# Two-layer graph network: another order of work between the layers, with the first block's layer-1 values in it

## The chip, the core and the metric

The kernel runs on one core of a Trainium2 chip. A core has a matrix engine (PE, with its weight loads listed as PEld), a vector engine (DVE), a scalar engine (ACT), a general engine (POOL) and a sync engine (SP) that only issues DMAs and waits. The metric is the time on the device in microseconds, the median of several runs.

## What is computed

Eight graphs ("batches") of 2048 nodes with 256 features share one 0/1 adjacency matrix. Cut to what matters, the reference is:

```python
# layer 0: attention in chunks of 256 keys, 4 heads of 64
h = relu(layernorm(x))
q, k, v = h @ Wq.T + bq, h @ Wk.T + bk, h @ Wv.T + bv
scores = clip(q @ k.T / 8, -10, 10); scores = where(adj == 0, -10, scores)
ctx = sum over chunks of softmax(scores within the chunk) @ v
o = ctx @ Wo.T + bo + h
x = x + layernorm(o) * gamma + beta
# layer 1: graph attention
h = relu(layernorm(x)); g = h @ W
e = leaky_relu(g @ a1 [:, None] + g @ a2 [None, :]); e = where(adj == 0, -1e9, e)
x = x + relu(softmax(e) @ g)
```

Everything is float32.

## The kernel before, in words

A batch is split into four blocks of 512 nodes, a block into four tiles of 128. Engines run their instructions in the order in which the program emits them (the schedule is written out by hand); waits between engines are put in where data, or a buffer's slot, is needed.

**Attention** of a batch is 32 steps, eight key chunks for each of the four query blocks. A step has two halves, `begin` and `end`, numbered 2f and 2f+1. Other work is hung on a half as a "piece" (`at(n, ...)`): pieces marked `first` run at its start, pieces marked `pe` at a set point among the matrix products, the others in between.

**A block between the layers** is the class `Between`: `output` and `take` (output projection, plus the residual), `stats`, `power`, `shift`, `scaled`, `gamma`, `add` (layer norm, then the sum into `x4`), then for layer 1 `stats1`, `power1`, `shift1`, `norm1` (layer norm and Relu), `turn1` and `keep1` (transposes on PE, copies by ACT into a tile `hT`), `values` and `keep` (the products with W and with a1 and a2; ACT copies them into `g`, DVE copies the two node values into `sd`). `ends(0)` is the two transposes with their copies, `ends(1)` the four value tiles with theirs. `beside` says at which half each of these runs for blocks 0 to 2; block 0 runs all of them within attention, block 1 (`low`) up to its transposes, block 2 (`mid`) up to `add`. The rest of `low` and `mid`, and all of block 3 (`last`), comes in the **layer change** after attention (lines 986 to 1066).

**The next batch's projections** (`ahead`, class `Projection`) share the layer change: for each of its blocks a load, `norm` (Relu on ACT), `turn` (transposes; the first copy by DVE, the second by ACT), `qk` (four groups of products, evicted by ACT) and `values` (two groups, evicted by DVE). The last batch has no next one. There the first products of layer 1 are taken early: `weights(i)` makes a group of four weight tiles on DVE (L758 and L764), `early(i)` multiplies them with `g` (L781).

**Layer 1** (`Layer1`) then runs 16 groups of weights and products: four target blocks times four groups of source tiles, with `finish` and `store` per block.

Buffers that matter here: in the layer change the small matrix results (`ps_m`) take four banks in turn, two called `n` and two called `t`; a bank is free once its result is evicted, by every reader. Tiles of normed rows (`hn`) have five slots, transposed ones (`hT`) two, per-block scales (`rn`) four.

The attention chain of the last block ends with a scaling on DVE (L470, `prod`) and a gather DMA from POOL (L475), behind which POOL still has the second `add` of block `mid` (L621) and a `beta` of `last` (L617).

Of the kernel before, what the change touches and what calls it, by code (L numbers as in the profile page):

```python
# [28 lines left out]
def gnn_two_layers(  # L29
# [18 lines left out]
    nc = tc.nc  # L48
# [7 lines left out]
    TB = NB // P  # L56
    NNB = N // NB
# [104 lines left out]
    def pe(piece):  # L162

        piece.kind = "pe"
        return piece
# [90 lines left out]
    def norm_stats(t4, mv, tiles):  # L256
        for t in tiles:
            stats = small.tile([P, 6], F32, tag="stats", name="stats")
            nc.vector.bn_stats(stats, t4[:, t, :])
            nc.vector.bn_aggr(mv[:, t, :], stats)  # L260
# [12 lines left out]
    def norm_tiles(tag, bufs):  # L273
        mv = small.tile([P, TB, 2], F32, tag="mv", name="mv")
        rn = small.tile([P, 2, TB], F32, tag=tag, name=tag, bufs=bufs)
        return mv, rn
# [19 lines left out]
    class Projection:  # L296
# [31 lines left out]
        def take(self, nb, c):  # L328
            if c == 0:
                nc.vector.tensor_copy(self.hT[nb][:, 0, :], self.pt.pop(c))  # L330
            else:
                nc.scalar.activation(self.hT[nb][:, 1, :], self.pt.pop(c), AF.Copy)
# [225 lines left out]
    class Between:  # L558
# [23 lines left out]
        def take(self, t2):  # L582
            if t2 == 0:
                self.o4 = work.tile([P, TB, F], F32, tag="o4", name="o4", bufs=1)
                self.mv, self.rn = norm_tiles("rn", 4)
            nc.vector.tensor_tensor(
                self.o4[:, 2 * t2:2 * t2 + 2, :], self.pp[t2].rearrange("p (i f) -> p i f", i=2),
                self.hn0[t2], op=ALU.add,
            )
# [32 lines left out]

        def stats1(self, tiles):
            if tiles[0] == 0:
                self.mv1, self.rn1 = norm_tiles("rn", 4)
            norm_stats(self.x4, self.mv1, tiles)

        def power1(self):
# [42 lines left out]
                    self.values(t)  # L671
                    self.keep(t)

        def beside(self):

            todo = {
                -3: [self.load],
                3: [lambda: self.residual(0)],
                4: [lambda: self.residual(1)],
                5: [lambda: self.bias(0)],  # L680
                6: [lambda: self.bias(1)],
                8: [pe(lambda: self.output(0)), pe(lambda: self.output(1)), lambda: self.beta(0)],
                9: [first(lambda: self.take(0)), first(lambda: self.take(1)), lambda: self.stats([0, 1])],
                10: [lambda: self.stats([2]), lambda: self.beta(1)],
                11: [lambda: self.stats([3])],
                12: [self.power],
                13: [self.shift],
                14: [lambda: self.scaled(range(TB))],
                15: [lambda: self.gamma(0)],
                16: [lambda: self.gamma(1)],  # L690
                18: [lambda: self.add(0)],
                20: [lambda: self.add(1)],
            }

            def at(n, *pieces):
                todo.setdefault(n, []).extend(pieces)

            if self.nb == NNB - 2:
                return todo
            for t in range(TB):  # L700
                at(21 + t, lambda t=t: self.stats1([t]))
            at(25, self.power1)
            at(26, self.shift1)
            at(27, lambda: self.norm1(0))
            at(28, lambda: self.norm1(1))
            if self.nb == 0:
                for c in range(FC):
                    at(32, pe(lambda c=c: self.turn1(c)))
                    at(33, first(lambda c=c: self.keep1(c)))
                for t in range(TB):  # L710
                    at(36 + t // 2 * 2, pe(lambda t=t: self.values(t)))
                    at(37 + t // 2 * 2, first(lambda t=t: self.keep(t)))
            return todo


    class Layer1:
# [37 lines left out]
        def weights(self, nb, j4):  # L754
            w = work.tile([P, 4, NB], F32, tag="e", name="w", bufs=5)
            for i in range(4):
                j = 4 * j4 + i
                nc.vector.tensor_scalar(  # L758
                    w[:, i, :], self.src[nb], self.cd[:, 0, j:j + 1], self.cd[:, 1, j:j + 1],
                    op0=ALU.mult, op1=ALU.max,  # L760
                )
                if i % 2:
                    two = w[:, i - 1:i + 1, :]
                    nc.vector.scalar_tensor_tensor(  # L764
                        two, bounds1[nb][:, j - 1:j + 1, :], 0.0, two, op0=ALU.is_gt, op1=ALU.mult
                    )
            return w
# [44 lines left out]
    STEPS2 = 2 * STEPS  # L812
# [91 lines left out]
    for b in range(B):  # L904
        sd = small.tile([P, 2, NT], F32, tag="sd", name="sd", bufs=2)
        sums = small.tile([P, NNB, FC], F32, tag="sums", name="sums", bufs=2)
        blocks = [Between(nb, projs[b], att, sd, sums) for nb in range(NNB)]
        low, mid, last = blocks[NNB - 3:]
        ahead = projs.get(b + 1)
        one = Layer1(b, blocks, sd, sums)  # L910
        pieces1 = [(nb, j4) for nb in range(NNB) for j4 in range(NT // 4)]
        ws, accs = {}, {}
        todo = {}

        def at(n, *pieces):
            todo.setdefault(n, []).extend(pieces)
# [4 lines left out]
        def early(i):  # L921
            one.products(accs[0], ws.pop(i), i)
# [2 lines left out]
            of[nb] = fetch_bounds(nb)  # L925

        for nb in range(NNB - 1):
            for n, pieces in blocks[nb].beside().items():
                at((nb + 1) * PER + n, *pieces)
        if b == 0:  # L930
            for n, pieces in once.items():
# [2 lines left out]
            for nb in range(NNB):  # L934
                n = 12 * nb + 5
# [20 lines left out]
        if ahead:  # L956
            at(STEPS2 - 14, lambda: ahead.load(0))
            at(STEPS2 - 13, lambda: ahead.load(1))
            at(STEPS2 - 11, lambda: ahead.norm(0, 0))
            at(STEPS2 - 10, lambda: ahead.norm(0, 1))  # L960
            for c in range(FC):
                at(STEPS2 - 2, pe(lambda c=c: ahead.put(0, c)))
                at(STEPS2 - 1, first(lambda c=c: ahead.take(0, c)))
            at(STEPS2 + 2, pe(lambda: ahead.tiles()), pe(lambda: ahead.qk(0, 0, ps_h)), lambda: ahead.norm(1, 0))
            at(STEPS2 + 3, pe(lambda: ahead.qk(0, 1, ps_h)), lambda: ahead.norm(1, 1))
        else:
            at(STEPS2 - 1, lambda: one.targets(0, TB))
            at(STEPS2, pe(lambda: one.sources(0)))
            at(STEPS2 + 3, lambda: weights(0))
        turn_about[0] = False  # L970
        for n in sorted(todo):
            if n < 4:
# [10 lines left out]
        assert not todo  # L983


        low.ends(1)
        if ahead:
            ahead.load(2)
            ahead.turn(1, 0)
            ahead.turn(1, 1)  # L990
        mid.stats1(range(TB))
        mid.power1()
        mid.shift1()
        if ahead:
            ahead.values(0)
        else:
            accs[0] = one.accumulators(0)
            early(0)
        mid.norm1(0)
        mid.norm1(1)  # L1000
        last.output(0)
        last.output(1)
        last.take(0)
        last.take(1)
        if ahead:
            ahead.norm(2, 0)
            ahead.norm(2, 1)
        else:
            one.targets(TB, 2 * TB)
            weights(1)  # L1010
        mid.ends(0)
        if ahead:
            ahead.qk(1)
        else:
            early(1)
        last.stats(range(TB))
        last.power()
        last.shift()
        last.scaled(range(TB))
        mid.ends(1)  # L1020
        if ahead:
            ahead.load(3)
            ahead.turn(2, 0)
            ahead.turn(2, 1)
            ahead.values(1)
        else:
            one.targets(2 * TB, 3 * TB)
            weights(2)
            early(2)
        last.adder = nc.vector  # L1030
        for t2 in range(2):
            last.gamma(t2)
            last.add(t2)
        last.stats1(range(TB))
        last.power1()
        last.shift1()
        if ahead:
            ahead.norm(3, 0)
            ahead.norm(3, 1)
            ahead.qk(2)  # L1040
        last.norm1(0)
        last.norm1(1)
        if ahead:
            ahead.values(2)
        last.ends(0)
        if ahead:
            ahead.turn(3, 0)
            ahead.turn(3, 1)
        last.ends(1)
        one.total()  # L1050
        if ahead:
            ahead.qk(3, 0)
            one.targets()
            one.sources(0)
            one.sources(1)
            ahead.qk(3, 1)
            weights(0)
            one.mean()
            weights(1)
            ahead.values(3)  # L1060
        else:
            one.targets(3 * TB, NT)
            one.sources(1)
            weights(3)
            one.mean()
            weights(4)

        far = projs[b + 2] = Projection(b + 2) if b + 2 < B else None
        for i, (nb, j4) in enumerate(pieces1):
# [19 lines left out]
            if far and i in (1, 3, 6, 9):  # L1089
                n = (1, 3, 6, 9).index(i)  # L1090
# [45 lines left out]
```

## Time and profile before

| what | value |
|---|---|
| median of three runs | 3699.47 us (3697.77 to 3701.71) |
| the profiled run | 3696.62 us, span of the core 3694.8 us |
| mean granted clock of PE | 0.995 |
| instructions | 99356 |
| attention of batch 1, from its first product after the layer-1 products (L416) to its last | 556.87 to 830.81 us |
| layer change, from the last attention product (L416) to the first layer-1 product (L781), batch 0 | 377.75 to 436.84 us |
| layer 1 of batch 0, first to last product | 436.84 to 555.20 us |

A line of the page's first part gives an engine's busy time, its share of the span and its instructions. A line of waits reads: the instruction that waited, by engine, output and line; whom it waited for; the total in us, how many times, and the longest. A line of the timeline reads: start, duration, engine, line, operation, output and inputs, shapes, how many merged, and in brackets the engine's idle time before it and who ended it. PE's ends are modelled, so two products that follow each other overlap in these lines; their starts are what counts.

### The profile page before, as it was taken

Reading aid. Unit: us, or ns where it says so; the run is one execution under the profiler, and the core shown is the slowest. Engines: PE = TensorE matmul, PEld = TensorE weight load, DVE = VectorE, ACT = ScalarE, POOL = GpSimd, SP = SyncE. Lnnn points to the kernel's source line nnn. Section 1 sums busy time; section 2 is a strip of 40 time slices with the busy share of each in tenths; the row PEclk is TensorE's granted clock in tenths of the full one; section 3 lists DMA queues with packets and bytes.
Section 4 is the critical chain, followed back from the end, with each engine's and each line's share of the span. In section 5 each row is a group of like instructions: output and inputs, shape, how many; then the busy total and the mean of one; then the engine's idle time right before and its main releaser. Section 6 shows DMA issues by size and latency. Waiting matters only on the chain.

```text
span 3694.8 us, 99356 instructions
## 1 busy us (share of the span) xinstructions
PE 3636.9 (98%) x43952; PEld 2166.4 (59%) x43952; DVE 2608.8 (71%) x3959; ACT 1940.4 (53%) x2879; POOL 1780.2 (48%) x1098
## 2 busy tenths in 40 slices
PE   8999999999999999999999999999999999999989
PEld 4444784447744477445774458654586445854458
DVE  4887577866777666775767757677576774767766
ACT  4777316773167632676236762377614766147640
POOL 0677016870177602785037750377404774048731
PEclk9999999999999999999999999999999999999999
DMA  4544113341133311343113331233312332123321
GB/s 142 134 127 106 45 52 82 82 104 29 64 82 88 93 42 50 84 101 77 46 49 85 93 75 46 64 80 84 78 60 52 88 82 58 46 58 82 76 52 35
DMA packets 116641, 274.83 MB, mean 74 GB/s; under 512 B 9968, under 2 KB 75248, under 8 KB 108016
## 3 DMA queue, kind: packets, MB, share of 16 engines
q0 software_dynamic: 32256, 117.45, 16.6%
q1 hardware_dynamic: 83952, 151.01, 11.9%
q8 instruction: 344, 5.64, 0.6%
q14 instruction: 89, 0.73, 0.1%
HBM read 130.03 MB, written 20.97 MB: 41 GB/s over the span
## 4 chain that ended last, share of the span: by engine, by line
PE 91%; DVE 5%; ACT 2%; issue 1%; DMA 1%; POOL 0%; POOLq 0%; SPq 0%; DVEq 0%; ACTq 0%
PE ps_s L400 23%; PE ps_n L416 22%; PE ps_s L781 12%; PE ps_n L781 6%; PE ps_t L781 6%; PE ps_t L428 6%; PE ps_t L577 3%; PE ps_s L344 2%; PE ps_t L651 2%; PE ps_t L358 2%; DVE e L440 2%; PE ps_n L358 2%; PE ps_n L344 1%; PE ps_t L344 1%; PE ps_t L292 1%
## 5 line engine op out<-in xcount | busy, mean ns | idle before, releaser
L455 POOL TENSOR_TENSOR both<-e 128x1024 f32<-128x1024 f32 x512 | 1216.2, 2400 | 772.8 <-PE ps_s L400 309.2
L440 DVE SCALAR_TENSOR_TENSOR e<-ps_s,bound 128x1024 f32<-128x1024 f32 x1024 | 1216.4, 1220 | 421.8 <-PE ps_s L400 416.7
L400 PE MATMUL ps_s<-q,k 64*32 64x512 f32 x16384 | 1364.0, 591 | 4.2 <-DVE e L440 3.0
L449 ACT ACTIVATE e<-e 128x1024 f32<-128x1024 f32 x1024 | 1053.1, 1050 | 579.0 <-DVE e L440 557.6
L416 PE MATMUL ps_n<-e,v 64*32 64x512 f32 x16384 | 1146.4, 590 | 1.2 <-DVE prod L470 1.1
L416 PEld LDWEIGHTS ps_n<-e,v 64*32 64x32 f32 x16384 | 430.9, 107 | 506.0 <-issue 439.7
L400 PEld LDWEIGHTS ps_s<-q,k 64*32 64x32 f32 x16384 | 419.7, 106 | 492.1 <-issue 343.0
L798 POOL TENSOR_TENSOR x<-x,r 128x256 f32<-128x256 f32 x128 | 98.5, 770 | 1081.2 <-DVE rz L791 1013.2
L428 PE MATMUL ps_t<-both,ones 64*32 64x512 f32 x4096 | 533.3, 591 | 1.3 <-SPq L372 1.2
L781 PE MATMUL ps_s<-g,w 128*128 128x257 f32 x2048 | 452.2, 382 | 8.2 <-DVE w L764 8.2
L781 PEld LDWEIGHTS ps_s<-g,w 128*128 128x128 f32 x2048 | 390.1, 191 | 65.1 <-issue 5.4
L470 DVE TENSOR_TENSOR prod<-ps_n,rz 128x512 f32<-128x512 f32 x448 | 288.4, 686 | 153.7 <-PE ps_n L416 97.4
L764 DVE SCALAR_TENSOR_TENSOR w<-bound,w 128x1024 f32<-128x1024 int8 x256 | 313.7, 1225 | 8.7
L758 DVE TENSOR_SCALAR w<-src,cd 128x512 f32<-128x512 f32 x512 | 270.9, 572 | 34.0 <-ACT src L752 33.2
L781 PE MATMUL ps_n<-g,w 128*128 128x257 f32 x1024 | 292.6, 382 | 0.0
L781 PE MATMUL ps_t<-g,w 128*128 128x257 f32 x1024 | 290.0, 380 | 0.0
L460 ACT ACTIVATE rz<-ps_t 128x512 f32<-128x512 f32 x256 | 152.6, 596 | 173.0 <-PE ps_t L428 107.9
L475 POOL DMA_DIRECT2D ctxT<-prod x224 | 193.8, 865 | 57.4 <-DVE sd L660 55.2
L781 PEld LDWEIGHTS ps_n<-g,w 128*128 128x128 f32 x1024 | 192.6, 190 | 43.4 <-issue 17.6
L781 PEld LDWEIGHTS ps_t<-g,w 128*128 128x128 f32 x1024 | 194.0, 189 | 28.0
L428 PEld LDWEIGHTS ps_t<-both,ones 64*32 64x32 f32 x4096 | 124.7, 106 | 101.0 <-SPq L372 49.1
L461 ACT ACTIVATE rz<-rz 128x512 f32<-128x512 f32 x256 | 161.4, 631 | 8.1
(125 smaller groups left out, 2844.8 us busy)
## 6 DMA issues: line engine op xcount, KB each, us to landing
ctxT<-prod POOLq DMA_DIRECT2D x224, 512.0 KB, 4.7
bound<-bound_d SPq DMA_DIRECT2D x60, 1024.0 KB, 5.1
xp<-in_x_dram SPq DMA_DIRECT2D x60, 512.0 KB, 4.7
rows<-in_adj_dram SPq DMA_DIRECT2D x32, 512.0 KB, 4.9
x<-in_x_dram SPq DMA_DIRECT2D x32, 512.0 KB, 5.1
out_dram<-x SPq DMA_DIRECT2D x31, 512.0 KB, 2.9
bound_d<-bound SPq DMA_DIRECT2D x4, 1024.0 KB, 6.2
out_dram<-x SPq DMA_DIRECT2D x4, 128.0 KB, 1.7
```

The lines of the kernel that those rows point to most:

```text
L400: nc.tensor.matmul(self.s[n, o][c * Q:(c + 1) * Q, kt, :], self.k[p][rows, at:at + Q], self.q[p][rows, nb * NB:(nb + 1) * NB], start=True, ...
L416: made.append(nc.tensor.matmul(self.num[n, c][h * Q:(h + 1) * Q, :], self.v[rows, j * KT + kt, at:at + Q], self.e[n, p][rows, i * KT + kt, :],
L428: nc.tensor.matmul(self.total[n][h * Q:(h + 1) * Q, :], ones[rows, :], self.both[n, h // 2][rows, h % 2, :], start=half == 1, stop=half == 0,)
L440: nc.vector.scalar_tensor_tensor(self.e[n, p][:, i * KT:(i + 1) * KT, :], self.s.pop((n, o)), -CLIP * SC, bounds[nb][:, j * KT:(j + 1) * K ...
L449: nc.scalar.activation(e, e, AF.Exp, scale=1.0 / SC)
L455: nc.gpsimd.tensor_tensor(self.both[n, p], e[:, 0], e[:, 1], op=ALU.add)
L461: nc.scalar.activation(rz, rz, AF.Exp, scale=-1.0)
L470: nc.vector.tensor_tensor(dst[:, c, :], self.num.pop((n, c)), self.rz[n], op=ALU.mult)
L475: nc.gpsimd.dma_start(self.ctxT[nb], self.prod.pop(n), accum_op=ALU.add)
L758: nc.vector.tensor_scalar(w[:, i, :], self.src[nb], self.cd[:, 0, j:j + 1], self.cd[:, 1, j:j + 1], op0=ALU.mult, op1=ALU.max,)
L764: nc.vector.scalar_tensor_tensor(two, bounds1[nb][:, j - 1:j + 1, :], 0.0, two, op0=ALU.is_gt, op1=ALU.mult)
L781: nc.tensor.matmul(accs[t][:, 0:F + 1], w[:, i, t * P:(t + 1) * P], g[:, j, :], start=j == 0, stop=j == NT - 1,)
```

## The change

It does the following:

- In batches 0 to 6 block 0's `norm1`, `turn1`, `keep1`, `values` and `keep` leave attention and come into the layer change as `zero.norm1`, `zero.ends(0)` and `zero.ends(1)`, between block `last`'s `norm1` and its `ends`. In the last batch they stay in attention.
- The layer change has another order. `mid.stats1` comes ahead of `low.ends(1)`, `mid.norm1` ahead of the next batch's values, and the q/k products of the next batch's blocks 1 and 2 are split, q and k apart. `gamma`, `add` and `stats1` of `last` come ahead of `mid.ends(1)`.
- In the last batch `weights(0)` leaves attention's half 67; the early products `early(0)` to `early(2)` come later, around `last`'s chain: the first after `mid.ends(1)`, the second after `last.norm1`, the third after `last.ends(1)`.
- The number of `rn` slots goes from four to eight.

Its core:

```diff
-                self.mv, self.rn = norm_tiles("rn", 4)
+                self.mv, self.rn = norm_tiles("rn", 2 * NNB)
...
-                self.mv1, self.rn1 = norm_tiles("rn", 4)
+                self.mv1, self.rn1 = norm_tiles("rn", 2 * NNB)
...
-        def beside(self):
+        def beside(self, values):
...
-            at(27, lambda: self.norm1(0))
-            at(28, lambda: self.norm1(1))
-            if self.nb == 0:
+            if self.nb == 1 or values:
+                at(27, lambda: self.norm1(0))
+                at(28, lambda: self.norm1(1))
+            if values:
...
-            for n, pieces in blocks[nb].beside().items():
+            for n, pieces in blocks[nb].beside(nb == 0 and not ahead).items():
...
-            at(STEPS2 + 3, lambda: weights(0))
...
```

The layer change, as emitted after it (the text of the new lines, the old ones are at 986 to 1066):

```python
last.adder = nc.vector
mid.stats1(range(TB))
low.ends(1)
mid.power1()
mid.shift1()
if ahead:
    ahead.load(2)
    ahead.turn(1, 0)
    ahead.turn(1, 1)
    mid.norm1(0)
    mid.norm1(1)
    ahead.norm(2, 0)
    ahead.values(0)
    last.output(0)
    last.output(1)
    last.take(0)
    last.take(1)
    ahead.norm(2, 1)
    ahead.load(3)
    mid.ends(0)
    last.stats(range(TB))
    ahead.qk(1, 0)
    last.power()
    last.shift()
    last.scaled(range(TB))
    ahead.qk(1, 1)
    for t2 in range(2):
        last.gamma(t2)
        last.add(t2)
    last.stats1(range(TB))
    mid.ends(1)
    last.power1()
    last.shift1()
    ahead.turn(2, 0)
    ahead.turn(2, 1)
    last.norm1(0)
    last.norm1(1)
    ahead.values(1)
    zero.norm1(0)
    zero.norm1(1)
    zero.ends(0)
    ahead.norm(3, 0)
    ahead.qk(2, 0)
    zero.ends(1)
    ahead.norm(3, 1)
    ahead.qk(2, 1)
    ahead.turn(3, 0)
    ahead.turn(3, 1)
    ahead.values(2)
    last.ends(0)
    last.ends(1)
    one.total()
    ...
else:
    mid.norm1(0)
    mid.norm1(1)
    one.targets(TB, 2 * TB)
    weights(0)
    mid.ends(0)
    last.output(0)
    last.output(1)
    last.take(0)
    last.take(1)
    mid.ends(1)
    last.stats(range(TB))
    last.power()
    last.shift()
    weights(1)
    last.scaled(range(TB))
    one.targets(2 * TB, 3 * TB)
    accs[0] = one.accumulators(0)
    early(0)
    for t2 in range(2):
        last.gamma(t2)
        last.add(t2)
    last.stats1(range(TB))
    last.power1()
    last.shift1()
    weights(2)
    last.norm1(0)
    last.norm1(1)
    early(1)
    last.ends(0)
    last.ends(1)
    early(2)
    one.total()
    ...
```

More of the change, by code (lines that the diff above doesn't have):

```diff
@@ L907, in gnn_two_layers @@
         blocks = [Between(nb, projs[b], att, sd, sums) for nb in range(NNB)]
-        low, mid, last = blocks[NNB - 3:]
+        zero, low, mid, last = blocks
         ahead = projs.get(b + 1)
@@ L983, in gnn_two_layers @@
         assert not todo
+        last.adder = nc.vector
+        mid.stats1(range(TB))
         low.ends(1)
+        mid.power1()
+        mid.shift1()
         if ahead:
@@ L990, in gnn_two_layers @@
             ahead.turn(1, 1)
[L991 to L994, printed above, removed]
+            mid.norm1(0)
+            mid.norm1(1)
+            ahead.norm(2, 0)
             ahead.values(0)
[L996 to L1006, printed above, removed]
-            ahead.norm(2, 1)
-        else:
-            one.targets(TB, 2 * TB)
-            weights(1)
@@ L1011, in gnn_two_layers @@
[L1011 to L1021, printed above, removed]
-            ahead.load(3)
+            last.output(0)
+            last.output(1)
+            last.take(0)
+            last.take(1)
+            ahead.norm(2, 1)
+            ahead.load(3)
+            mid.ends(0)
+            last.stats(range(TB))
@@ L1023, in gnn_two_layers @@
+            ahead.qk(1, 0)
+            last.power()
+            last.shift()
+            last.scaled(range(TB))
+            ahead.qk(1, 1)
+            for t2 in range(2):
+                last.gamma(t2)
+                last.add(t2)
+            last.stats1(range(TB))
+            mid.ends(1)
+            last.power1()
+            last.shift1()
             ahead.turn(2, 0)
             ahead.turn(2, 1)
+            last.norm1(0)
+            last.norm1(1)
             ahead.values(1)
[L1026 to L1037, printed above, removed]
+            zero.norm1(0)
+            zero.norm1(1)
+            zero.ends(0)
             ahead.norm(3, 0)
+            ahead.qk(2, 0)
+            zero.ends(1)
             ahead.norm(3, 1)
[L1040 to L1044, printed above, removed]
@@ L1045, in gnn_two_layers @@
-        last.ends(0)
-        if ahead:
+            ahead.qk(2, 1)
             ahead.turn(3, 0)
             ahead.turn(3, 1)
-        last.ends(1)
-        one.total()
-        if ahead:
+            ahead.values(2)
+            last.ends(0)
+            last.ends(1)
+            one.total()
             ahead.qk(3, 0)
@@ L1061, in gnn_two_layers @@
         else:
+            mid.norm1(0)
+            mid.norm1(1)
+            one.targets(TB, 2 * TB)
+            weights(0)
+            mid.ends(0)
+            last.output(0)
+            last.output(1)
+            last.take(0)
+            last.take(1)
+            mid.ends(1)
+            last.stats(range(TB))
+            last.power()
+            last.shift()
+            weights(1)
+            last.scaled(range(TB))
+            one.targets(2 * TB, 3 * TB)
+            accs[0] = one.accumulators(0)
+            early(0)
+            for t2 in range(2):
+                last.gamma(t2)
+                last.add(t2)
+            last.stats1(range(TB))
+            last.power1()
+            last.shift1()
+            weights(2)
+            last.norm1(0)
+            last.norm1(1)
+            early(1)
+            last.ends(0)
+            last.ends(1)
+            early(2)
+            one.total()
             one.targets(3 * TB, NT)
```

## The prediction

> **What bounds the kernel now.** I read the page first. The matrix engine is busy almost throughout, and the chain that ended last is nearly all its own.
>
> ```profile
> PE 3636.9 (98%) x43952; PEld 2166.4 (59%) x43952; DVE 2608.8 (71%) x3959; ACT 1940.4 (53%) x2879; POOL 1780.2 (48%) x1098
> PE 91%; DVE 5%; ACT 2%; issue 1%; DMA 1%; POOL 0%; POOLq 0%; SPq 0%; DVEq 0%; ACTq 0%
> ```
>
> So three things can move the time: PE's idle time, its clock, and how densely its instructions follow each other. The second view is PE's waits (total us, times, longest).
>
> ```profile
> PE ps_t L358 <- ACT q L348: 13.2, 7, 1.9
> PE ps_s L781 <- DVE w L764: 8.2, 4, 3.5
> PE ps_n L651 <- DVE prod L470: 3.9, 1, 3.9
> PE ps_t L292 <- DVE sd L660: 3.4, 7, 0.5
> ```
>
> The two waits that come seven times are in the layer change of batches 0 to 6, once each; the other two are in the last batch. Third, the windows around the first 1.9 us wait (columns: length, busy time of five engines, granted clock, DMA).
>
> ```profile
> 407.90:411.30 3.40, 3.40 (x9) 1.52 (x8) 3.00 (x10) 0.12 (x1) 0.00 (x0) 1.00 0.01 2
> 411.30:414.70 3.40, 1.51 (x5) 0.56 (x4) 0.16 (x1) 3.37 (x8) 0.00 (x0) 1.00 0.01 2
> 414.70:418.10 3.40, 3.40 (x10) 2.69 (x9) 0.34 (x1) 3.24 (x7) 0.00 (x0) 0.50 0.47 154
> ```
>
> After a window with PE idle for 1.89 us, the next one runs at half clock: 1.7 us lost. From the last attention product to the first layer-1 product the change takes 59.09 us in batch 0, but 57.40 us in batches 2 and 3, where the same wait straddles two windows. So five of seven changes pay 1.69 us more.
>
> Fourth, attention, by the start of the last group of denominator products in each step (timeline, batch 1).
>
> ```profile
> 717.02 0.61 PE L428 MATMUL ps_t<-both,ones 64*32 64x512 f32 x4
> 725.41 0.61 PE L428 MATMUL ps_t<-both,ones 64*32 64x512 f32 x4
> 733.13 0.61 PE L428 MATMUL ps_t<-both,ones 64*32 64x512 f32 x4
> 742.55 0.61 PE L428 MATMUL ps_t<-both,ones 64*32 64x512 f32 x4
> 750.27 0.61 PE L428 MATMUL ps_t<-both,ones 64*32 64x512 f32 x4
> 760.18 0.61 PE L428 MATMUL ps_t<-both,ones 64*32 64x512 f32 x4
> 770.09 0.61 PE L428 MATMUL ps_t<-both,ones 64*32 64x512 f32 x4
> ```
>
> A bare step is 7.72 us. The step to 725.41, in which block 0's second `norm1` runs, is 8.39; the step with its transposes (to 742.55) 9.42; the two with its values 9.91 each. All batches show these within 0.03 us.
>
> [...] 1.89 us idle in a 3.40 us window is enough here, while 1.65 us (3560.16 to 3561.81) was not: the boundary lies between. [...] eight 128x128 transposes take 8 x 0.109 = 0.87 us in a row in the layer change, but lengthen an attention step of 64x32 tiles by 1.69; eight value products take 1.74 there and lengthen a step by 2.19. [...] at 411.18 ACT's Ln ends an 8.4 us wait on DVE, and the q evictions behind it start only at 413.58; that is the 1.9 us wait.
>
> **The change, part by part.** I lay the new order over the first change's clock. Spacings from the timeline: four transposes 0.43, one value tile 0.87, eight L358 or L577 products 1.73, one q/k half of a part 1.72; on ACT a Relu 0.52, hT copy 0.58, q/k eviction 0.57; on DVE statistics of a tile 0.53.
>
> (1) Attention, batches 0 to 6. Block 0's `norm1`, transposes and values leave: 0.66 + 1.69 + 2 x 2.19 = 6.73 us a batch, all on PE's path.
>
> (2) The same work in the change: transposes 0.87 + values 3.47 = 4.34 us of PE.
>
> (3) Waits that go. Counted from PE's issue rather than the modelled end: 0.64 us before 401.00 (PE waits for `sd`, behind ACT's four scalings) and 2.04 before 414.30, together 2.68. The second goes since the q evictions now stand ahead of `last.power1`, and the first key half before the statistics finish.
>
> (4) Waits that come. `mid.stats1` is put ahead of `low.ends(1)`. DVE runs in order and its third tile needs POOL's second addition, which stands behind the last gather:
>
> ```profile
> 377.88 1.29 DVE L470 TENSOR_TENSOR prod<-ps_n,rz 128x512 f32<-128x512 f32 x2 [12.25 <-PE ps_n L416]
> 379.28 0.16 DVE L660 COPY sd<-ps_t 128x2 f32<-128x2 f32 x1
> 379.47 0.87 POOL L475 DMA_DIRECT2D ctxT<-prod  x1 [7.20 <-DVE sd L660]
> 380.07 1.57 POOL L621 TENSOR_TENSOR x<-x,o 128x512 f32<-128x512 f32 x1
> 381.35 0.60 PE L292 MATMUL ps_t<-ident,hn 128*128 128x128 f32 x4
> ```
>
> The addition ends at 381.64; two tiles of statistics follow; the `sd` copy that frees the first value bank ends at 382.92 instead of 379.44. The transposes of `ahead` reuse that bank (four turn about), so they start at 382.98 instead of 381.34: **1.64 us**. Bounds: 0, if the addition comes sooner; 2.75, if the first tile waits for it too.
>
> Next, `mid.ends(1)`'s `sd` copies stand behind `last.stats1`. Second output at 389.02, so take 390.95, statistics to 393.87; ACT evicts q at 395.26, then Ln and Exp, DVE shift, scalings from 396.60; gamma and add 397.76 to 400.49 (2.73, as at 406.19); `stats1` to 402.71, first `sd` 402.77. PE has finished block `mid`'s values at 401.97: **0.86**. Bounds 0.3 and 1.9 (gamma waiting for all four scalings).
>
> Then ACT's eight Relus of `last` and `zero` run 404.45 to 408.59, while PE has the value products only until 407.14; its four transposes follow the Relus: **1.25**, in gaps of 0.4. Last, `last.ends(0)` is followed by `last.ends(1)` with nothing between: as in the last batch now, where transposes at 3586.76 should give values at 3587.19 and the first value tile ends 0.76 late: **0.76**. Sum 4.51.
>
> (5) Half clock. Of the new waits only the first comes near the boundary, when it lies in one window, which half its positions allow. I take one to two of seven changes, 2.2 us, against 8.5 before.
>
> Batches 0 to 6: 7 x (-6.73 + 4.34 - 2.68 + 4.51) = -3.9, -8.5 + 2.2: **-10.2 us**.
>
> (6) Last batch. `weights(0)` leaves the front of DVE's queue, where it held the scaling at 3543.59 and so the value tiles. But `mid.ends(0)` now comes straight after `low.ends(1)`: counted from 3539.31, PE is done at 3.65 and waits for `mid.norm1` (addition 3.95, statistics 5.1, shift 5.9, Relus to 8.1): 4.15 us plus some 1.2 of half clock. Outputs to 13.3, `mid` values 16.8, `early(0)` 23.7, `early(1)` 30.7: their weights (10.3 and 24.95) are in time, which removes these:
>
> ```profile
> 3562.25 7.21 PE L781 MATMUL ps_s<-g,w 128*128 128x257 f32 x32 [2.08 <-DVE w L764]
> 3576.42 10.06 PE L781 MATMUL ps_s<-g,w 128*128 128x257 f32 x32 [3.48 <-DVE w L764]
> ```
>
> `last`'s statistics and `weights(1)` let its Relus end at 32.9: 1.92 us wait, then 0.76, with half clock about even odds (0.9). `early(2)` fills PE to 45.5 while `weights(3)` (4.35 us each) finishes; source transposes and mean to 46.8, the fourth product group to 53.7. Now it ends at 3603.42 - 3539.31 = 64.1. **-10.4 us.** The later 1.8 us wait of L748 I leave at -0.
>
> (7) At nothing: the two larger `rn` counts (memory only); the adder set earlier (its calls come later in both); q/k in two parts (same instructions); SP's two loads, issued at 371.74 and 372.54 and landed by 377.25, before the change begins, held by nothing that moves. POOL and SP get no new instruction.
>
> Sum: -10.2 - 10.4 = -20.6 on a span of 3694.8. That run took 3696.62; the three timed ones 3697.77 to 3701.71. The median 3699.47 gives **3679 us**.
>
> **Rivals.**
> A, as worked: 3679, own range 3672 to 3688, chance 0.52.
> B, every change is halved in clock: the first wait is a little over 1.7 us and always counted. 5.7 more x 1.69 = +9.7: 3689. For: 1.64 against a boundary between 1.65 and 1.89. Against: a straddled wait isn't counted (batches 2 and 3). 0.15.
> C, half of the new waits hide (Relus or statistics faster released than I lay out): -15.8, no half clock: 3661. For: each is a difference of two long queues. Against: the POOL addition has a fixed place. 0.20.
> D, the slower side: waits on parts of a tile are waits on the whole tile. Then `mid.stats1` holds DVE from its first tile (2.75 instead of 1.64, with half clock for sure, +2.5) and gamma waits for all scalings (+1.06, half clock in part, +0.7): 4.3 x 7 + 1 = +31, 3710. It decides from +2.9 a change. Against: at 3594.99 products start on half a weight tile. 0.07.
> E, the last batch gains nothing since its vector chain still ends last: 3689. Against: in my layout the weights lead. 0.06.
>
> **Range and chances.** 3660 to 3694 holds A, nearly all of B and E, and most of C. A measurement can tell about 0.2% (7.4 us) from none: faster means below 3692.1. A and C, most of B and E: 0.80; the rest of B and E, and the edges of A and D: 0.12; D, and a wait I have missed: 0.08.
>
> **What would show it.** Steps 8.39, 9.42 and 9.91 of block 0 become 7.72 in batches 0 to 6. PE L292 waits for DVE `sd` twice a change, about 1.5 and 0.7 us by modelled ends, and for ACT `hn`; the wait of L358 on `q` is gone; the change takes about 63.6 us instead of 57.4 or 59.1. In the last batch PE L292 waits about 4 us on `hn`. Wrong if the change takes over 67 us, or if attention's steps stay long.

## The result, and the profile after

The changed kernel takes 3688.17 us (median of four runs, 3684.12 to 3688.98); the kernel before, beside it, 3700.59 (four runs, 3697.77 to 3703.28). The ratio is 0.9964, with a 95% interval of 0.9947 to 0.9982: 12.4 us or 0.34% faster. The prediction was 3679, range 3660 to 3694. The two profiled executions lie nearer to each other, 3694.8 and 3687.1 us of span (the first was below all four timed executions of the kernel before, the second is the slowest of the changed one); sums below are made on these.

Busy time of each engine, on the page of the changed kernel:

```profile
PE 3633.1 (99%) x43952; PEld 2202.9 (60%) x43952; DVE 2600.7 (71%) x3959; ACT 1946.7 (53%) x2879; POOL 1781.4 (48%) x1098
```

PE does as many products as before (43952). PE's busy time fell by 3.8 us and its idle time by the other 3.9. PE's waits in the changed kernel (total us, times, longest):

```profile
PE ps_t L292 <- DVE sd L660: 14.5, 14, 1.4
PE ps_t L292 <- ACT hn L283: 11.9, 29, 2.8
PE ps_t L651 <- ACT hT L644: 2.7, 8, 0.3
PE ps_s L749 <- ACT r L795: 1.3, 1, 1.3
```

The wait of L358 on `q` (13.2 us) is gone, and so are the waits of the layer-1 products on their weights in the last batch (8.2 us). Waits on `sd` come twice in each of seven layer changes. Of the 29 on `hn`, ten are in the start-up, as before; two in each layer change and five in the last batch are new, and so is one on `hT` in each layer change. In the trace of the kernel before, the granted clock falls to half for stretches of 3.41 us or twice that (414.71 to 418.13, 3575.45 to 3582.28); a window is a stretch of about that length. The windows around the first wait of batch 0's change, and those from the end of the longest one in the last batch on (length, busy time of five engines, granted clock, DMA):

```profile
377.90:381.30 3.40, 2.00 (x13) 1.89 (x14) 2.20 (x10) 1.76 (x5) 1.31 (x2) 1.00 0.61 116
381.30:384.70 3.40, 3.40 (x17) 3.00 (x16) 1.38 (x2) 2.67 (x6) 0.00 (x0) 1.00 0.00 0
...
3548.20:3551.60 3.40, 3.01 (x10) 2.04 (x11) 3.33 (x6) 2.95 (x9) 0.00 (x0) 0.50 0.01 2
3551.60:3555.00 3.40, 3.40 (x10) 2.65 (x9) 0.74 (x2) 0.47 (x2) 0.00 (x0) 0.50 0.00 0
```

In none of the seven changes does the clock fall any more; in the last batch two windows in a row are halved. Steps of batch 1's attention, from the timeline of the changed kernel:

```profile
717.39 0.61 PE L428 MATMUL ps_t<-both,ones 64*32 64x512 f32 x4
725.78 0.61 PE L428 MATMUL ps_t<-both,ones 64*32 64x512 f32 x4
733.51 0.61 PE L428 MATMUL ps_t<-both,ones 64*32 64x512 f32 x4
741.23 0.61 PE L428 MATMUL ps_t<-both,ones 64*32 64x512 f32 x4
748.96 0.61 PE L428 MATMUL ps_t<-both,ones 64*32 64x512 f32 x4
756.68 0.61 PE L428 MATMUL ps_t<-both,ones 64*32 64x512 f32 x4
```

Block 0's transposes and values no longer lengthen their steps (7.72 us each). But the first interval, 8.39 us, which I had put down to block 0's `norm1`, is as long as before, although that `norm1` is not there any more.

The layer change's first wait, in the timeline of the changed kernel:

```profile
376.43 1.56 POOL L621 TENSOR_TENSOR x<-x,o 128x512 f32<-128x512 f32 x1
...
376.83 1.03 PE L651 MATMUL ps_n<-w1s,hT 128*128 128x258 f32 x4
...
378.03 0.43 DVE L259 BATCH_NORM_STATS2 stats<-x 128x6 f32<-128x256 f32 x1 [1.43 <-POOL x L621]
...
379.11 0.13 DVE L660 COPY sd<-ps_t 128x2 f32<-128x2 f32 x1
...
379.30 0.66 PE L292 MATMUL ps_t<-ident,hn 128*128 128x128 f32 x4 [1.43 <-DVE sd L660]
```

DVE stops at the third tile until POOL's addition ends at 377.99; the `sd` copy comes after two tiles of statistics. PE's last value tile ends issuing at 376.83 + 0.87 = 377.70, so PE loses 1.60 us. The other three:

```profile
397.50 1.03 PE L651 MATMUL ps_n<-w1s,hT 128*128 128x258 f32 x4
...
399.17 0.66 PE L292 MATMUL ps_t<-ident,hn 128*128 128x128 f32 x4 [0.64 <-DVE sd L660]
...
400.79 4.03 ACT L283 ACTIVATE hn<-x,rn 128x256 f32<-128x256 f32 x8
401.83 1.89 PE L358 MATMUL ps_n<-wvT,hT 128*128 128x256 f32 x8
...
404.38 0.33 PE L292 MATMUL ps_t<-ident,hn 128*128 128x128 f32 x1 [0.16 <-ACT hn L283]
404.87 0.33 PE L292 MATMUL ps_t<-ident,hn 128*128 128x128 f32 x1 [0.16 <-ACT hn L283]
405.04 0.60 PE L292 MATMUL ps_n<-ident,hn 128*128 128x128 f32 x4
...
421.54 1.28 PE L651 MATMUL ps_t<-w1s,hT 128*128 128x258 f32 x4 [0.34 <-ACT hT L644]
```

Counted from PE's issue, these are 399.17 - 398.37 = 0.80 us for `mid.ends(1)`'s `sd` copies; 1.05 for the Relus, as block 0's first four transposes are done at 405.04 instead of 403.99; and 0.76 for the values behind the last block's copies (the next value tile starts at 422.65 instead of 421.89). With the first, 4.21 us.

Where the time went, on the two profiled executions (each batch cut at the start of its last attention product and its first and last layer-1 product; the prediction counted the change from that product's end, some 0.6 us later, so its 63.6 us stands beside 63.2 in that count):

| part | predicted, us | measured, us |
|---|---|---|
| attention, batches 0 to 6 | -47.1 | -32.5 |
| layer change without half clock, seven times | +43.2 | 7 x (63.80 - 57.99) = +40.7 |
| half clock in the changes | -6.3 | 5 x 1.69 = -8.5 |
| last batch, from its last attention product to its last layer-1 product | -10.4 | 150.63 to 140.84: -9.8 |
| start-up, last attention, layer 1 elsewhere | 0 | +2.4 |
| sum | -20.6 | -7.7 |

### The profile page after: what moved, and what is told of

Read it like the earlier page. It is cut to its first block, busy times and chain, and to the rows that moved or that the text cites. A ratio compares the mean times of both kernels' runs of the same rounds, so it can differ in the third digit from the quotient of the medians.

```text
span 3687.1 us, 99355 instructions
## 1 busy us (share of the span) xinstructions
PE 3633.1 (99%) x43952; PEld 2202.9 (60%) x43952; DVE 2600.7 (71%) x3959; ACT 1946.7 (53%) x2879; POOL 1781.4 (48%) x1098
## 4 chain that ended last, share of the span: by engine, by line
PE 90%; DVE 5%; ACT 2%; issue 1%; DMA 1%; POOL 1%; SPq 0%; POOLq 0%; DVEq 0%; ACTq 0%
PE ps_s L400 23%; PE ps_n L416 22%; PE ps_s L782 11%; PE ps_n L782 6%; PE ps_t L428 6%; PE ps_t L782 6%; PE ps_t L577 3%; PE ps_s L344 2%; PE ps_n L344 2%; PE ps_t L344 2%; DVE e L440 2%; PE ps_t L358 1%; PE ps_n L358 1%; PE ps_t L292 1%; PE ps_t L651 1%
## 5 line engine op out<-in xcount | busy, mean ns | idle before, releaser
L440 DVE SCALAR_TENSOR_TENSOR e<-ps_s,bound 128x1024 f32<-128x1024 f32 x1024 | 1218.7, 1219 | 399.7 <-PE ps_s L400 397.3
L400 PE MATMUL ps_s<-q,k 64*32 64x512 f32 x16384 | 1398.5, 591 | 4.2 <-DVE e L440 3.0
L416 PE MATMUL ps_n<-e,v 64*32 64x512 f32 x16384 | 1182.5, 590 | 2.2 <-DVE prod L470 2.2
L416 PEld LDWEIGHTS ps_n<-e,v 64*32 64x32 f32 x16384 | 449.0, 107 | 501.6 <-issue 417.9
L400 PEld LDWEIGHTS ps_s<-q,k 64*32 64x32 f32 x16384 | 432.8, 106 | 478.2 <-issue 324.7
L470 DVE TENSOR_TENSOR prod<-ps_n,rz 128x512 f32<-128x512 f32 x448 | 288.3, 685 | 164.5 <-PE ps_n L416 94.8
```

The lines of the kernel that those rows point to most:

```text
L400: nc.tensor.matmul(self.s[n, o][c * Q:(c + 1) * Q, kt, :], self.k[p][rows, at:at + Q], self.q[p][rows, nb * NB:(nb + 1) * NB], start=True, ...
L416: made.append(nc.tensor.matmul(self.num[n, c][h * Q:(h + 1) * Q, :], self.v[rows, j * KT + kt, at:at + Q], self.e[n, p][rows, i * KT + kt, :],
L440: nc.vector.scalar_tensor_tensor(self.e[n, p][:, i * KT:(i + 1) * KT, :], self.s.pop((n, o)), -CLIP * SC, bounds[nb][:, j * KT:(j + 1) * K ...
L470: nc.vector.tensor_tensor(dst[:, c, :], self.num.pop((n, c)), self.rz[n], op=ALU.mult)
```

## The experiments

Each kernel was timed in five rounds beside the kernel before; "against before" is the ratio of their times with its interval. The theory at the start was that the sum above is made of independent parts, and that each wait comes from an instruction standing in the wrong place of one engine's queue. Lengths of attention, change and last batch are of each run's one profiled execution.

### The last batch alone, and the others alone

In the changed kernel, the layer change of batches 0 to 6 is put back as it was before (its lines from `low.ends(1)` to `ahead.values(3)`, under `if ahead`), and the last batch keeps its new lines:

```diff
-            for n, pieces in blocks[nb].beside(nb == 0 and not ahead).items():
+            for n, pieces in blocks[nb].beside(nb == 0).items():
...
-        last.adder = nc.vector
-        mid.stats1(range(TB))
-        low.ends(1)
-        mid.power1()
-        mid.shift1()
         if ahead:
+            low.ends(1)
             ahead.load(2)
             ahead.turn(1, 0)
             ahead.turn(1, 1)
+            mid.stats1(range(TB))
+            mid.power1()
+            mid.shift1()
+            ahead.values(0)
...
         else:
+            last.adder = nc.vector
+            mid.stats1(range(TB))
+            low.ends(1)
+            mid.power1()
+            mid.shift1()
             mid.norm1(0)
             mid.norm1(1)
```

> The last batch in the new order, batches 0 to 6 as before. Theory (the gains of the two parts add up, and most of the 12.4 us is the last batch's): from the last attention product to the last layer-1 product of the last batch 140.8 us instead of 150.6, waits of 3.9, 2.1 and 3.5 us gone and one of about 2.8 us on the Relus in their place; the total falls by 9.8 us, to about 3691. Rival (the gain is batches 0 to 6, and the last batch is only shifted): under 4 us.

Against before 0.9975 (0.9966 to 0.9984), -9.2 us. From last attention product to last layer-1 product 140.98 us. Its waits:

```profile
PE ps_t L358 <- ACT q L348: 13.2, 7, 1.9
PE ps_t L292 <- ACT hn L283: 9.1, 12, 2.9
```

The seven waits on `q` are still there, those on the weights have gone, as expected. This kernel has the eight `rn` slots with the old layer change, and its changes take 59.67 or 57.98 us, as before: the slots alone do nothing that shows. Four of the seven changes are halved in clock here, five in the kernel before, with the same order of work: in the other three the wait lies across two windows, with 1.41 to 1.77 us in the fuller one.

The other half has the two branches the other way round, with `weights(0)` back in attention's half 67:

> Batches 0 to 6 in the new order, the last batch as before. Theory: attention 5.6 us a batch shorter, the layer change 63.8 us instead of 59.7 or 58.0 (4.1 or 5.8 longer, by whether a half-clock window fell into it), together some -2.6 to -7 us: 3694 to 3698. Rival (my prediction's size): -10 us, 3690.

Against before 1.0001 (0.9993 to 1.0009): nothing, with room for -3 us at most. Attention of batches 1 to 6 averages 268.7 us against 273.6 in the kernel before, the change takes 63.80 us in all seven. Its last batch takes 152.01 us where the kernel before has 150.63, with four half-clock windows in it instead of three, so some 1.4 us of the total are not of batches 0 to 6. So the whole measurable gain of the change is the last batch's; in batches 0 to 6 it takes 5 us from attention and gives 4.1 or 5.8 back in the layer change. Both my sizes failed here: the prediction's -10 us, and even -2.6 is at the edge of the interval.

### What made the wait on q, and the half clock

The kernel before, with four lines moved:

```diff
-        last.power1()
-        last.shift1()
         if ahead:
             ahead.norm(3, 0)
             ahead.norm(3, 1)
             ahead.qk(2)
+        last.power1()
+        last.shift1()
```

> The kernel before, with block last's power1 and shift1 put behind qk(2), so that ACT evicts q and k before it waits for DVE's statistics. Theory (ACT's order alone made the 1.9 us wait, and that wait alone the half-clock windows): the wait of L358 on q goes in all seven changes and no half-clock window is left in them, at most 0.3 us of waiting on the last block's Relus comes instead; -14 for the wait, -8 for the clock, about -20 us: 3680. Rival 1 (the wait moves to the last block's Relus): -8 or less. Rival 2 (the half-clock windows come from elsewhere): five of them stay.

Against before 0.9943 (0.9929 to 0.9956), -21.1 us. The change takes 55.83 us in all seven batches, instead of 57.99 or 59.68, and no half-clock window falls into any of them. The waits of this kernel (L358 on `q` is no longer among them):

```profile
PE ps_s L781 <- DVE w L764: 8.2, 4, 3.5
PE ps_t L292 <- ACT hn L283: 6.8, 11, 1.5
...
PE ps_n L651 <- DVE prod L470: 3.9, 1, 3.9
PE ps_t L292 <- DVE sd L660: 3.4, 7, 0.5
```

So ACT's order was the cause: it stood at the Ln of `last.power1`, waiting for DVE's statistics (8.4 us in batch 0 of the kernel before), with the q and k evictions ready behind it. Two calls moved behind them gain more than the whole change, 21 us against 12 (the two intervals still overlap a little). None of the eleven waits on `hn` lies in batches 0 to 6's changes (seven are in the start-up, four in the last batch): the small wait on the last block's Relus that the expectation allowed for did not come.

### Taking the new waits apart

First only the first one, in batches 0 to 6:

```diff
-        mid.stats1(range(TB))
+        mid.stats1([0, 1] if ahead else range(TB))
         low.ends(1)
+        if ahead:
+            mid.stats1([2, 3])
```

> The changed kernel, with the third and fourth tile of mid.stats1 behind low.ends(1) in batches 0 to 6. Theory (the sd copies stand behind two tiles of statistics that wait for POOL's addition): the first wait of PE L292 on DVE sd (1.43 us by modelled ends, 1.64 by issue) goes in all seven changes, each change takes 62.2 us instead of 63.8, the total falls by 11 us from the changed kernel, to about 3677. Rival (mid's chain, now 0.5 us later, takes the wait's place at its transposes): no gain.

Against before 0.9939 (0.9927 to 0.9952), about 9 us faster than the changed kernel's 0.9964. The change takes 62.15 us, 1.65 less, and the waits on `sd` are halved:

```profile
PE ps_t L292 <- ACT hn L283: 11.9, 29, 2.8
...
PE ps_t L292 <- DVE sd L660: 4.5, 7, 0.6
```

Then all four, the other three by these lines on top of the split:

```diff
             for t2 in range(2):
                 last.gamma(t2)
                 last.add(t2)
+            mid.ends(1)
             last.stats1(range(TB))
-            mid.ends(1)
+            zero.norm1(0)
+            zero.norm1(1)
             last.power1()
             last.shift1()
...
             ahead.values(1)
-            zero.norm1(0)
-            zero.norm1(1)
             zero.ends(0)
...
-            ahead.turn(3, 0)
-            ahead.turn(3, 1)
             ahead.values(2)
             last.ends(0)
+            ahead.turn(3, 0)
+            ahead.turn(3, 1)
             last.ends(1)
```

> The changed kernel, with the four waits of its layer change taken apart in batches 0 to 6: the third and fourth tile of mid.stats1 behind low.ends(1); mid.ends(1) ahead of last.stats1; zero.norm1 ahead of last.power1; turn(3) between last.ends(0) and last.ends(1), behind values(2). Theory (each of the four, 1.64, 0.84, 1.25 and 0.57 us, has its own cause in an engine's order): the layer change takes 59.5 us instead of 63.8, -30 us from the changed kernel, a ratio of 0.988 to the kernel before. Rival (waits come back at the next point, since ACT and DVE are as full as PE there): half of it or less.

Against before 0.9890 (0.9877 to 0.9904), -40.7 us. The change takes 59.62 us, 4.18 less than 63.80, where the four waits read from the timeline sum to 4.21. In the list of waits the layer changes of batches 0 to 6 are gone:

```profile
PE ps_t L292 <- ACT hn L283: 8.7, 12, 2.8
...
PE ps_n L651 <- DVE prod L470: 1.5, 1, 1.5
PE ps_n L416 <- DVE prod L470: 1.5, 2, 0.8
```

What is left of `hn` is start-up and the last batch. Nothing came back at the next point. So the other three are shown as a group; the Relus' part is also seen alone in the next experiment.

### Block 0: in attention or in the change

The changed kernel without `zero.norm1`, `zero.ends(0)` and `zero.ends(1)`, and with `beside(nb == 0)`, so that block 0 stays in attention in all batches:

> The changed kernel, with block 0's norm1, transposes and values left in attention in all batches (its calls taken out of the layer change). Theory (moving them is even: the step of block 0's norm1 stays 8.39 us and the step after its values grows by 0.43, so attention gives 5.6 us a batch, and the layer change pays 4.34 us of products and 1.25 us of waiting on the Relus): attention 5.6 us longer, the layer change 58.2 us instead of 63.8, the total within 3 us of the changed kernel. Rival (my prediction's sizes, 6.73 from attention): 8 us slower than the changed kernel.

Against before 0.9963 (0.9949 to 0.9977), the same as the changed kernel. Attention of batches 1 to 6 averages 273.7 us instead of 268.9, the change 58.44 instead of 63.80. Moving block 0 is even: 4.8 us saved, 5.36 paid (4.34 of products, and 1.02 beside the 1.05 read for the wait on the Relus), and the half-clock windows, absent in this kernel's changes too, do not depend on it.

The same in the kernel without the four waits:

> no_waits, with block 0's norm1, transposes and values left in attention. Theory (moving block 0 pays once the layer change has no waits[...]): attention 5.6 us longer, the layer change 55.3 us instead of 59.6, together 1.3 us a batch or 9 us slower than no_waits, a ratio of 0.9915 to the kernel before. Rival (the move is worth nothing by itself, only the order): equal to no_waits, 0.989.

Against before 0.9907 (0.9891 to 0.9924), beside 0.9890 with block 0 moved. The intervals overlap, so the total doesn't decide; the parts do: the change is 55.24 us instead of 59.62 (in the seventh 56.00), attention 273.8 instead of 268.7. That is 0.7 us a batch for the move, half of the 1.3 expected (5.6 against 4.34), since attention gives 5.1 and not 5.6.

### The step of 8.39 us

Block 0's statistics for layer 1 lie in halves 37 to 40, block 1's `take` and `stats` in 41 to 43, all on DVE. In the changed kernel, batches 0 to 6:

```diff
+            later = 8 if self.nb == 0 and not values else 0
             for t in range(TB):
-                at(21 + t, lambda t=t: self.stats1([t]))
-            at(25, self.power1)
-            at(26, self.shift1)
+                at(21 + later + t, lambda t=t: self.stats1([t]))
+            at(25 + later, self.power1)
+            at(26 + later, self.shift1)
```

> The changed kernel, with block 0's stats1, power1 and shift1 eight halves later in batches 0 to 6. Theory (the step of 8.39 us comes from these statistics on DVE, which lie in the same halves as block 1's take and stats and hold up the clips behind them, and never came from norm1): that step is 7.72 us in batches 0 to 6 and the later one of 8.39 us, block 1's, stays; -0.66 us a batch, -4.6 in all. Rival (block 1's own statistics make it): it stays 8.39.

Against before 0.9951 (0.9939 to 0.9964), beside the changed kernel's 0.9964; the intervals overlap, so the total doesn't decide. The steps of batch 1 do:

```profile
709.08 0.61 PE L428 MATMUL ps_t<-both,ones 64*32 64x512 f32 x4
...
716.80 0.61 PE L428 MATMUL ps_t<-both,ones 64*32 64x512 f32 x4
...
724.62 0.61 PE L428 MATMUL ps_t<-both,ones 64*32 64x512 f32 x4
```

716.80 to 724.62 is 7.82 us where it was 8.39. In batches 1 to 6 this step is 7.80 to 8.06; in the last batch, where the statistics were not moved, it is 8.39, and so is block 1's later step everywhere. So the cause is block 0's layer-1 statistics, moved here with their `power1` and `shift1`. The traces point to DVE: in the step of 8.39 us PE's loads for the scores wait 1.4 us for DVE's clips (L440), in the bare step behind it 0.3, and in this run's step not at all (batch 1). Over all steps the gain is small: 1 to 31 of batches 1 to 6 average 263.0 us here, and 262.6 over this run and the two below that move the statistics too, against 263.2 where they stay. The 0.1 to 0.3 us left in the step come with a new wait: in all six batches DVE's scaling (L470) waits 0.93 to 1.11 us in it for the gather to land, and in the changed kernel's 8.39 us steps not at all.

### The last batch in yet another order

```diff
             one.targets(TB, 2 * TB)
-            weights(0)
-            mid.ends(0)
+            ws[0] = one.weights(0, 0, part=range(2))
             last.output(0)
             last.output(1)
             last.take(0)
             last.take(1)
-            mid.ends(1)
+            mid.ends(0)
             last.stats(range(TB))
             last.power()
             last.shift()
-            weights(1)
             last.scaled(range(TB))
+            one.weights(0, 0, ws[0], range(2, 4))
+            mid.ends(1)
...
             last.shift1()
-            weights(2)
+            weights(1)
             last.norm1(0)
             last.norm1(1)
-            early(1)
             last.ends(0)
             last.ends(1)
+            weights(2)
+            early(1)
             early(2)
```

together with the two edits before it (the four waits, the statistics):

> no_waits and stats_elsewhere together, and another order for the last batch: last.output ahead of mid.ends(0), half of weights(0) ahead of the outputs and half behind last.shift, early(1) and early(2) behind last.ends(1). Theory: -4.6 us for attention's step; in the last batch 136 to 138 us from the last attention product to the last layer-1 product instead of 140.8, since the last block's chain starts some 5 us sooner; -8 us from no_waits. Rival (the wait moves to the last block's Relus and costs as much): -4.6 alone.

Against before 0.9879 (0.9865 to 0.9892). The last batch takes 141.86 us, no less than the 141.62 of the kernel without the four waits, and not the 136 to 138 expected. The rival holds, only its place is another:

```profile
PE ps_t L292 <- ACT hn L283: 7.3, 14, 1.5
...
PE ps_t L577 <- DMA ctxT<-prod: 2.7, 1, 2.7
```

The outputs now wait 2.7 us for the last gather to land, and the Relus of the last block still cost 1.8: four of the 14 waits on `hn`, the longest 1.27 (the 1.5 of this line is in the start-up). As a control, the same two edits with the last batch as in the changed kernel:

> no_waits and stats_elsewhere together, the last batch as in the changed kernel. Theory (last_too's order of the last batch gained nothing, its first wait only changed from the Relus to the gather's landing): equal to last_too within 2 us, the step of 8.39 us at 7.8 to 8.0. Rival (that order gained some of its 4.6 us): 2 to 4 us slower than last_too.

Against before 0.9879 (0.9864 to 0.9894): the same. Its last batch takes 140.97 us. Differences of a microsecond mean little here: the changed kernel's order of the last batch takes 139.25 to 140.97 us in the four runs in which one half-clock window falls into it, and 140.77 to 141.62 in the four with two. By these ratios this kernel is some 45 us faster than the kernel before and 31 us faster than the changed one, by order alone (and the slots of `rn`).

## Why the prediction was right, and which terms were mis-sized

**Total.** 3688.17 lies in the range, just above case A's own upper end; the direction held, the size was 12.4 instead of 20.6 us. That it lies at the 3689 of cases B and E is chance: neither every change was halved nor did the last batch gain nothing. And the direction rests on the last batch alone: the -10.2 us forecast for batches 0 to 6 did not come, and the wide range covered that.

**Attention, step (1), was the term that was mis-sized.** Predicted 6.73 us a batch; 5.0 came (steps 1 to 31 of batches 1 to 6 average 268.2 us in the five kernels with block 0 in attention and 263.2 in the four with it moved and the statistics left where they were). Three things are in it. The transposes and values gave 1.69 + 2 x 2.18, as said; why they lengthen a step by more than they take in a row (0.87 and 1.74) is not shown by any run. The 0.66 us of the 8.39 us step did not come: I tied it to `norm1` because it lay in the same step, but the step is as long without it, and shrinks when the statistics move. And the step behind the values, which holds the next block's outputs, went from 11.62 to 12.04: behind the values it had been shorter, and I had not counted that. Of the last 0.6 us, 0.35 lies in the three shortened steps and the one between them, which average 7.73 to 7.87 us where a bare one is 7.72. In the long ones of these DVE's scaling waits for the previous gather to land, as here in a step of 8.50 us of batch 4 (timeline of the changed kernel):

```profile
2110.16 1.29 DVE L470 TENSOR_TENSOR prod<-ps_n,rz 128x512 f32<-128x512 f32 x2 [1.30 <-DMA ctxT<-prod]
```

That a longer step had hidden such late landings is my reading; no run tests it.

**The waits that go, step (3), were right**, cause and size: ACT's order, shown by moving two calls; 55.83 us against 57.99 is 2.16 for the wait (2.04 said).

**The waits that come, step (4), were right** in place and cause, all four: 1.60, 0.80, 1.05 and 0.76 us where 1.64, 0.86, 1.25 and 0.76 were said, and they went when the instructions ahead of them were moved: the first by itself, the other three together. Case D is refuted by the timeline: the statistics of tiles 0 and 1 ran at 375.44 and 375.99, before POOL's addition had ended at 377.99, so here the wait is on the part of the tile. Case C too: no wait was missing.

**Half clock, step (5).** I allowed for 2.2 us, an estimate of one to two changes at the 1.69 us measured; none came, and case B is out. The allowance mixed two counts: the 1.64 us was counted from PE's issue, the 1.65 and 1.89 of the boundary from modelled ends, where this wait is 1.43. But the boundary itself isn't a rule either. In the kernel before, a window with PE idle for 1.81 us (3609.6 to 3613.0, the wait of L748) was not followed by half clock, and in the last batch of the kernel with `power1` behind `qk(2)` one with 1.96 was not, though 1.89 was each time in the layer changes:

```profile
3553.72:3557.13 3.41, 1.45 (x7) 0.93 (x5) 1.37 (x5) 1.29 (x5) 0.00 (x0) 1.00 0.00 0
3557.13:3560.54 3.41, 1.89 (x9) 1.71 (x10) 3.34 (x5) 0.00 (x0) 0.00 (x0) 1.00 0.00 0
```

So PE's idle time in a window does not alone decide; what does stays open. That the wait on `q` made the half clock of the layer changes is shown by its removal, not by a boundary.

**The last batch, step (6)**: -9.8 against -10.4. The wait on the Relus is 3548.54 - 3545.53 = 3.0 us to the first transpose, and 4.3 to the end of the fourth beyond their own 0.43, where 4.15 was said. Two half-clock windows followed where I had priced one. The second came although PE was idle for only 0.39 us in the window before it, and four of the seven other runs with this order of the last batch have one window only; why is open. `early(0)` and `early(1)` ran through (3560.01, 64 products in 14.04 us), and the two later waits came at 3574.71 and 3577.29. That the later wait of L748 would not change was wrong by 0.5 us (1.8 to 1.3).

**What I did not see** is that the four new waits, 4.2 us a batch, were a matter of order and not of the move: they ate most of what the removed wait, its half clock and attention gave, and only the Relus' 1.05 of them goes when block 0 stays in attention.

## What to carry to other kernels

When work is moved between stages, write down for each engine which instruction now stands ahead of one that frees a bank, and when its own input arrives: the wait on `q` (1.89 us) and the four new ones (1.60, 0.80, 1.05 and 0.76) were found and priced that way, and went when a call or two was moved for each. Charge a longer step to an instruction only if a neighbouring step with the same instruction shows it too; lying in the same half is not enough. A wait of PE can cost more than its length: the 1.89 us on `q` cost another 1.69 of half clock in five of seven changes, the first new one, 1.43 by the same count, none in seven; so the longest one goes first.

## What the runs showed that I had not expected

- The order of two calls, against the kernel before, is worth 21 us; all order together, with the same products, 45 us (1.2%).
- What other products added to an attention step differed with the step ahead: one with output products took 12.04 us behind a bare step and 11.62 behind one with value products. Why is not shown.
- A window with 1.96 us of idle PE passed without half clock (last batch, `power1` behind `qk(2)`), where those with 1.89 in five layer changes of the kernel before did not.
- DVE's copies of 128x2 values, 0.13 to 0.15 us long, started 0.05 to 0.07 us apart after the first new wait (379.11, 379.16, 379.22, 379.29), so the backlog of four took 0.33 us.
